# Edge loops of a graph network hand over means in rows of all channels, in place of numerators and denominators

## The chip, the core and the metric

The kernel runs on one core of a Trainium2 chip. The core has five engines with an instruction stream each: TensorE (PE, with its weight loads PEld), VectorE (DVE), ScalarE (ACT), GpSimd (POOL) and SyncE (SP). They work side by side and wait for one another by semaphores. SP issues the ordinary DMAs, POOL the indirect ones that gather rows by index. Time is device microseconds of one execution; lower is better.

## What is computed

10,000 nodes and 160,000 edges with 64 channels each. Four layers of a message-passing network (GENConv with a softmax over the incoming edges of each node, by channel), then one attention layer. What matters here, cut from the reference:

```python
def _genconv(x, src, dst, ea, W1, b1, lg, lb, W2, b2, t):
    m = jax.nn.relu(x[src] + ea) + EPS
    logits = m * t
    mx = jax.ops.segment_max(logits, dst, num_segments=N)
    e = jnp.exp(logits - mx[dst])
    denom = jax.ops.segment_sum(e, dst, num_segments=N)
    alpha = e / denom[dst]
    agg = jax.ops.segment_sum(m * alpha, dst, num_segments=N)
    h = agg + x
    ...
# attention, per edge, 8 heads of 8 channels
score = Kh[src] * Qh[dst] * inv_sqrt_d * Eh
score = jnp.exp(jnp.clip(score.sum(-1, keepdims=True), -5.0, 5.0))
wV = jax.ops.segment_sum(Vh[src] * score, dst, num_segments=n)
```

The edges come sorted by destination, so the edges of a node are neighbours.

## The kernel before

**Layout.** Edges stand along the free dimension, channels on partitions. The edge list is cut in two halves: the first half runs forwards on partitions 0 to 63, the second backwards on 64 to 127. A chunk is 512 columns (`CE`), four groups of 128 columns (`G`), so 1024 edges; there are 158 chunks, the last three short (256, 256 and 128 columns).

**A softmax layer** (`softmax_layer`, four of them; layer 0 also transposes the edge attributes and counts edges per node) goes through the chunks in a loop. Its parts:

- `fetch(k + 3)`: SP loads the marks (two DMAs), and in layers 1 to 3 the edge attributes `ea` (one).
- `front(k)`: POOL gathers the source nodes' rows into `xg`, eight gathers (seven chunk buffers). PE adds edge attributes and gathered rows in a PSUM bank `z`. ACT makes the logits `lg` in two steps (L834, L835). DVE scans them for the running maximum `u` (L841) and subtracts (L843). ACT makes `up` and `e` in three steps (L846, L848, L849).
- `back(k - 1)`, for the chunk before: DVE makes `me` (L869) and scans the running sums `se` of the exponentials (the denominators, L871) and `sm` of the weighted messages (the numerators, L874). Two transposes in blocks of 32x32 (L900) put both in a tile `so`. SP stores it in four DMAs (L904) to the table `st0` in DRAM.
- `decay(k)`: ACT writes `dec` (L856), one PSUM bank, which the scans of `back(k)` read; so it waits for the scan `sm` of chunk k - 1.

At the last edge of each node the running sums are that node's sums; so the table holds a row for every edge, and one row is read for each node. Row 2e + s of `st0` belongs to edge column e of side s and holds 32 denominators and 32 numerators of channels 0 to 31, then the same of channels 32 to 63: 512 bytes, stored in pieces of 256.

`InOrder` ties each engine's instructions to one another in the order in which they are written, so nothing overtakes on an engine.

**The node layer** (`node_layer`) follows each edge loop. `fetch` gathers the rows of 128 nodes a time (79 gathers, in groups of up to eight) by the row numbers `ends`; `divide` forms numerator / denominator as numerator x exp(-ln(denominator)) with two ACT operations and a DVE multiply; `enter` transposes to channels on partitions and adds the layer's input. Then follow two matrix products and two norms, in a software pipeline of groups. `rows_of_nodes` works out `ends` once, during layer 0.

**The attention layer** (`attention_layer`) runs the same chunk loop once more: eight gathers `kv` a chunk, a query scan, scores, weights, a scan `s` (L1201), one transpose to `so` (L1212) and four stores (L1216) to `st1`, in pieces of 128 bytes. Per chunk SP issues eight DMAs there. After it the result rows are gathered from `st1`.

In the layers 1 to 3 the `z` of a chunk lies in one of five PSUM banks; in layer 0 in one of three. `oe` is a bank that the edge loops of layers 1 to 3 use only at their last chunk.

Of the kernel before, what the change touches and what calls it, by code (L numbers as in the profile page):

```python
# [9 lines left out]
F32 = mybir.dt.float32  # L10
# [16 lines left out]
def kernel(ctx: ExitStack, tc: tile.TileContext, a, out):  # L27
# [75 lines left out]
    tables = [dram.tile([NP, D], F32, name=f"table{i}") for i in range(L)]  # L103
    kv_table = dram.tile([NP, D2], F32, name="kv_table")
    qs = dram.tile([2 * HALF + NP + P, D], F32, name="qs")
    st0 = dram.tile([2 * HALF + 1, D2], F32, name="st0")
    st1 = dram.tile([2 * HALF + 1, D], F32, name="st1")

    ends_d = dram.tile([2, HALF], BF, name="ends_d")
    keeps_d = dram.tile([2, HALF], BF, name="keeps_d")  # L110
# [59 lines left out]
    empty = const.tile([1, D2 + D], F32, name="empty")  # L170
    for h in range(2):
        nc.gpsimd.memset(empty[:, h * D:h * D + 32], 1.0)
        nc.gpsimd.memset(empty[:, h * D + 32:(h + 1) * D], -EPS)
    nc.gpsimd.memset(empty[:, D2:], 0.0)
    zeros = const.tile([P, 500], F32, name="zeros")
    nc.gpsimd.memset(zeros, 0.0)
    later.append((st0[2 * HALF:2 * HALF + 1, :], empty[:, 0:D2]))
    later.append((st1[2 * HALF:2 * HALF + 1, :], empty[:, D2:]))

    def load(name, shape, ap):  # L180
        t = const.tile(shape, F32, name=name)
# [314 lines left out]
    def rows_of_nodes(pool, ph):  # L496

        def t(name):
            return pool.tile([P, NT], F32, name="rn_" + name, bufs=1)
        V = nc.vector  # L500
        cnt = t("cnt")
        V.tensor_copy(cnt, ph)
        upto, before = place_nodes(pool, cnt, "ept")
        some = t("some")
        V.tensor_scalar(some, cnt, 0.0, None, op0=OP.is_gt)
        ra, rb, inb = t("ra"), t("rb"), t("inb")
        V.tensor_scalar(inb, before, float(HALF), None, op0=OP.is_ge)
# [36 lines left out]
    def pairs(n):  # L544
        return (n + 1) // 2
# [253 lines left out]

    V, S = nc.vector, nc.scalar  # L800

    def softmax_layer(l, ea_rows=None):

        prev = {}
# [60 lines left out]
        def back(k, z, u, dec, e):  # L865
# [11 lines left out]
            if k == NC - 1:  # L877
# [15 lines left out]
                for i, t in ((1, se), (2, sm)):  # L893
                    V.tensor_mul(far[:, i:i + 1], far[:, i:i + 1], top[:, 3:4])
                    V.scalar_tensor_tensor(t[:D, m - 1:m], fin[:D, i:i + 1], top[:, 2:3],
                                           far[:, i:i + 1], op0=OP.mult, op1=OP.add)

            so = edge.tile([P, CE // 32, 2, 32], F32, name="so", bufs=3)
            for i, t in ((0, se), (1, sm)):
                V.transpose(so[:, :m // 32, i, :], t[:, :m].rearrange("p (b e) -> p b e", e=32))  # L900
# [14 lines left out]
        for k in range(NC):  # L915
# [18 lines left out]
            if l == 1 and k % 4 == 0:  # L934
                clear_queries(k // 4)
            order()
        back(NC - 1, *held)
        order()

    def node_layer(l):  # L940
# [21 lines left out]
        @stage  # L962
# [138 lines left out]

        for g in range(3):
            fetch(g)
        divide(0)
        for i in range(NG2 + (4 if last else 3)):
            span_narrow(i - 3)
            widen(i - 1)
# [5 lines left out]
            spans(i - 1)  # L1113
            relu_narrow(i - 3)
            square(i - 2)
            divide(i + 1)
            back(i - 3)
            root_wide(i - 1)
            leave(i - 3)
# [14 lines left out]
    def attention_layer():  # L1134
# [60 lines left out]
        def back(k, keep, pv, sc):  # L1195
# [8 lines left out]
            if k == NC - 1:  # L1204
# [6 lines left out]
            so = edge.tile([P, CE // 32, 32], F32, name="so1", tag="so", bufs=3)  # L1211
            V.transpose(so[:, :m // 32, :], s[:, :m].rearrange("p (b e) -> p b e", e=32))  # L1212
            rows_out = st1[2 * g0 * G:2 * (g0 + n) * G, :].rearrange(
                "(b e s) (h c) -> s h e b c", e=32, s=2, h=2)
            for q in range(4):
                nc.sync.dma_start(rows_out[q // 2, q % 2], so[q * 32:(q + 1) * 32, :m // 32])  # L1216

        order = InOrder()
        got = [fetch(k) for k in range(2)]
# [2 lines left out]
        for k in range(NC):  # L1222
            kvs = fetch_kv(k)
            if k + 2 < NC:
                got.append(fetch(k + 2))
            pv, psc = scores(k, kvs, made)
            if held is not None:
                back(k - 1, *held)
            held = got[k][0], pv, weights(k, psc)
            if k + 1 < NC:  # L1230
                made = ahead(k + 1, *got[k + 1])
            order()
        back(NC - 1, *held)
        order()

    puts = []
# [69 lines left out]
```

## Time and profile before

| | us |
|---|---|
| median of three runs | 10168.21 (10164.5 to 10176.87) |
| profiled execution, its own time | 10256.79 |
| its span, first to last instruction | 10254.7 |
| softmax layer 0, first to last `lg` on ACT | 176 to 2001 |
| softmax layer 3, last `lg` | 7986 |
| attention, first to last gather | 8301 to 10111 |
| a gather on POOL (L756) | 0.943 busy, 0.30 between two |
| DVE scans of a full chunk | 1.28, 1.27, 1.26 |
| DVE transposes of a full chunk | 0.69, 0.67 |
| ACT operations of a full chunk | 0.55 to 0.75 |
| DMA queue of SP | 2,247,039 packets, 827 MB |

The profile's page gives each engine's busy time, the idle time ahead of each group of instructions with what ended it ("releaser"; "remote" where the profile doesn't know, "issue" where it sees no wait), and the DMA traffic. In the timeline a line holds start, duration, engine, source line, operation, output and inputs, and in brackets the idle time of the engine just before it with its releaser. 67,417 instructions ran.

### The profile page before, as it was taken

Reading aid. Unit: us, or ns where it says so; the run is one execution under the profiler, and the core shown is the slowest. Engines: PE = TensorE matmul, PEld = TensorE weight load, DVE = VectorE, ACT = ScalarE, POOL = GpSimd, SP = SyncE. Lnnn points to the kernel's source line nnn. Section 1 sums busy time; section 2 is a strip of 40 time slices with the busy share of each in tenths; the row PEclk is TensorE's granted clock in tenths of the full one; section 3 lists DMA queues with packets and bytes.
Section 4 is the critical chain, followed back from the end, with each engine's and each line's share of the span. In section 5 each row is a group of like instructions: output and inputs, shape, how many; then the busy total and the mean of one; then the engine's idle time right before and its main releaser. Section 6 shows DMA issues by size and latency. Waiting matters only on the chain. (4 is left out here: it accounts for less than half of the span.)

```text
span 10254.7 us, 67417 instructions
## 1 busy us (share of the span) xinstructions
PE 4014.2 (39%) x15762; PEld 2685.3 (26%) x15762; DVE 5449.4 (53%) x7473; ACT 2805.0 (27%) x4803; POOL 6358.1 (62%) x6760
## 2 busy tenths in 40 slices
PE   3554445443333333433333343333333444444452
PEld 2333333222222221222222221222222233333331
DVE  3777677535555554355555543555555445545453
ACT  2333333333333333333333342333333310000000
POOL 4566666556666665566666646666666456666665
PEclk6666666665555556665666575555555667777776
DMA  3555555524555554244444433444444235555553
GB/s 89 113 125 123 123 124 123 123 59 119 125 125 129 128 124 109 62 102 105 104 104 103 105 78 71 105 105 104 103 104 106 62 92 122 125 123 126 122 128 82
DMA packets 2462634, 1103.63 MB, mean 108 GB/s; under 512 B 2039472, under 2 KB 2254438, under 8 KB 2462239
## 3 DMA queue, kind: packets, MB, share of 16 engines
q1 hardware_dynamic: 2247039, 827.14, 33.8%
q0 software_dynamic: 215200, 272.11, 12.6%
q8 instruction: 140, 2.29, 0.1%
q14 instruction: 255, 2.09, 0.1%
HBM read 626.51 MB, written 471.91 MB: 107 GB/s over the span
## 5 line engine op out<-in xcount | busy, mean ns | idle before, releaser
L756 POOL DMA_INDIRECT xg<-table,idxA x2500 | 2358.6, 943 | 1916.9 <-remote 829.7
L756 POOL DMA_INDIRECT xg<-table,idxB x2500 | 2358.8, 944 | 763.1 <-issue 761.2
L841 DVE TENSOR_TENSOR_SCAN u<-lg,u,marks 128x512 f32<-128x512 f32 (+1 forms) x628 | 798.5, 1272 | 2721.5 <-ACT lg L835 1612.7
L829 PE MATMUL z<-ea,eencW 128*128 128x512 f32 (+1 forms) x892 | 864.3, 1071 | 2137.1 <-DMA ea<-eaT 898.3
L831 PEld LDWEIGHTS z<-ident,xg 128*128 128x128 f32 x3512 | 800.4, 311 | 591.8 <-issue 566.5
L756 POOL DMA_INDIRECT kv<-kv_table,idxA x625 | 589.5, 943 | 439.7 <-remote 220.2
L831 PE MATMUL z<-ident,xg 128*128 128x128 f32 x3512 | 794.5, 395 | 162.0 <-DMA xg<-table,idxB 85.9
L829 PEld LDWEIGHTS z<-ea,eencW 128*128 128x128 f32 x892 | 222.2, 306 | 2231.8 <-issue 1981.7
L871 DVE TENSOR_TENSOR_SCAN se<-dec,se,e 128x512 f32<-128x512 f32 (+1 forms) x628 | 792.2, 1261 | 0.0
L874 DVE TENSOR_TENSOR_SCAN sm<-dec,sm,me 128x512 f32<-128x512 f32 (+1 forms) x628 | 782.3, 1246 | 0.0
L846 ACT ACTIVATE up<-lg 128x512 f32<-128x512 f32 (+1 forms) x632 | 374.3, 592 | 1352.9 <-issue 693.6
L756 POOL DMA_INDIRECT kv<-kv_table,idxB x625 | 589.7, 944 | 191.1 <-issue 190.2
L834 ACT ACTIVATE lg<-z 128x512 f32<-128x512 f32 (+1 forms) x446 | 249.4, 559 | 1555.8 <-remote 1032.3
L1185 PE MATMUL dec<-eq,head_sum 128*128 128x512 f32 (+2 forms) x316 | 237.1, 841 | 931.2 <-DVE eq L1183 887.1
L1192 ACT ACTIVATE sc<-sc 128x512 f32<-128x512 f32 (+1 forms) x158 | 98.7, 625 | 1744.7 <-DVE sc L1191 685.0
L784 PE MATMUL ept<-ident,er 128*64 128x128 f32 x1250 | 269.3, 380 | 752.4 <-ACT ea L788 517.7
L856 ACT ACTIVATE dec<-up 128x512 f32<-128x512 f32 (+1 forms) x632 | 377.1, 597 | 658.8 <-issue 561.0
L756 POOL DMA_INDIRECT n_g<-st,ends x316 | 300.8, 952 | 403.2 <-issue 142.2
L835 ACT ACTIVATE lg<-lg,teps,tcol 128x512 f32<-128x512 f32 (+1 forms) x632 | 471.4, 746 | 21.1
L829 PE MATMUL hist<-ea,eencW 128*128 128x512 f32 x186 | 189.5, 1123 | 709.5 <-DMA ea<-eaT 286.6
L829 PE MATMUL ept<-ea,eencW 128*128 128x512 f32 x186 | 185.5, 1100 | 710.3 <-DMA ea<-eaT 286.4
L1156 DVE TENSOR_TENSOR_SCAN qh<-marks,qh,oe 128x512 f32<-128x512 bf16 (+1 forms) x157 | 198.6, 1265 | 488.6 <-remote 389.8
(285 smaller groups left out, 8704.9 us busy)
## 6 DMA issues: line engine op xcount, KB each, us to landing
st<-so SPq DMA_DIRECT2D x2480, 128.0 KB
ea<-eaT SPq DMA_DIRECT2D x620, 256.0 KB
marks<-ends_d SPq DMA_DIRECT2D x1240, 64.0 KB
st<-so SPq DMA_DIRECT2D x652, 64.0 KB
xg<-table,idxA POOLq DMA_INDIRECT x2500
xg<-table,idxB POOLq DMA_INDIRECT x2500
qs<-zeros SPq DMA_DIRECT2D x40, 1000.0 KB
er<-in_edge_attr_dram SPq DMA_DIRECT2D x310, 128.0 KB
```

The lines of the kernel that those rows point to most:

```text
L756: nc.gpsimd.indirect_dma_start(out=t, out_offset=None, in_=table, in_offset=bass.IndirectOffsetOnAxis(ap=idx, axis=0))
L784: nc.tensor.matmul(pt[:D, g * G:(g + 1) * G], er[:, 0, g, :], ident, start=True, stop=True)
L829: nc.tensor.matmul(z[:, :m], eencW, ea[:, :m], start=True, stop=False)
L831: nc.tensor.matmul(z[:, g * G:(g + 1) * G], xg[:, g, :, :].rearrange("p s d -> p (s d)"), ident, start=False, stop=(g == n - 1))
L834: S.activation(lg[:, :m], z[:, :m], AF.Relu)
L835: S.activation(lg[:, :m], lg[:, :m], AF.Identity, bias=teps[:, l:l + 1], scale=tcol[:, l:l + 1])
L841: V.tensor_tensor_scan(u[:, 1:m + 1], lg[:, :m], marks[:, :m], last, op0=OP.max, op1=OP.add)
L846: S.activation(up[:, :m], lg[:, :m], AF.Relu)
L856: S.activation(dec[:, :m], up[:, :m], AF.Exp, scale=-1.0)
L871: V.tensor_tensor_scan(se[:, :m], dec[:, :m], e[:, :m], prev.get("e", zero1), op0=OP.mult, op1=OP.add)
L874: V.tensor_tensor_scan(sm[:, :m], dec[:, :m], me[:, :m], prev.get("m", zero1), op0=OP.mult, op1=OP.add)
L1185: nc.tensor.matmul(psc[:, :m], head_sum, eq[:, :m], start=True, stop=True)
```

## The change

The tables `st0` and `st1` hold rows of all 64 channels, 256 bytes each. Chunks, sides, 32 columns and 16 blocks of a chunk (`SB`) number the rows so that, for one side and one place within the blocks, the 16 blocks of a chunk are 16 neighbouring rows: a run of 4 KB. A chunk is stored in two DMAs, one for each side, of 32 such runs.

The mean leaves the edge loop: `mean` computes exp(-ln(`se`)) on ACT (into the bank `oe`, in layer 0 into SBUF) and multiplies it with `sm` on DVE, then transposes the product. `send_sums` copies, on ACT, the upper 32 channels of each side from their partitions to those of the lower 32, so that a partition holds whole rows, and issues the stores. In iteration k, `send` handles chunk k - 3 and `mean` chunk k - 2, both ahead of `back(k - 1)`. In attention only `send` is there. `divide` disappears from the node layer, whose gathers are 256 bytes a row. `rows_of_nodes` translates `ends` into the new row numbers. A spare part of the tables holds the rows for nodes without edges.

```diff
-    st0 = dram.tile([2 * HALF + 1, D2], F32, name="st0")
-    st1 = dram.tile([2 * HALF + 1, D], F32, name="st1")
+    NB = -(-HALF // CE)
+    SB = CE // 32
+    st0 = dram.tile([NB * 64 * SB, D], F32, name="st0")
+    st1 = dram.tile([NB * 64 * SB, D], F32, name="st1")
...
+        part, upper_part = pool.tile([P, NT], I32, name="rn_part", bufs=1), t("upper")
+        place = t("place")
+        V.tensor_single_scalar(part, ends, 10, op=OP.logical_shift_right)
+        V.tensor_scalar(place, part, float(64 * SB), None, op0=OP.mult)
+        for down, keep, times in ((0, 1, 32 * SB), (1, 31, SB), (6, SB - 1, 1)):
+            of = ends
+            if down:
+                V.tensor_single_scalar(part, ends, down, op=OP.logical_shift_right)
+                of = part
+            V.tensor_single_scalar(part, of, keep, op=OP.bitwise_and)
+            V.tensor_copy(upper_part, part)
+            V.scalar_tensor_tensor(place, upper_part, float(times), place, op0=OP.mult, op1=OP.add)
+        V.tensor_copy(ends, place)
...
+    def turn_sums(t, m):
+        so = edge.tile([P, SB, 2, 32], F32, name="so", bufs=3)
+        V.transpose(so[:, :m // 32, 0, :], t[:, :m].rearrange("p (b e) -> p b e", e=32))
+        return so
+
+    def send_sums(k, so, st):
+        g0, n = chunks[k]
+        nb, b0 = n * G // 32, g0 * G // 32 % SB
+        rows_of = st.rearrange("(k s e b) d -> k s e b d", s=2, e=32, b=SB)[g0 * G // CE]
+        for s in range(2):
+            p = s * D
+            S.activation(so[p:p + 32, :nb, 1, :], so[p + 32:p + D, :nb, 0, :], AF.Copy)
+            nc.sync.dma_start(rows_of[s, :, b0:b0 + nb, :],
+                              so[p:p + 32, :nb].rearrange("p b h c -> p b (h c)"))
...
-            so = edge.tile([P, CE // 32, 2, 32], F32, name="so", bufs=3)
-            for i, t in ((0, se), (1, sm)):
-                V.transpose(so[:, :m // 32, i, :], t[:, :m].rearrange("p (b e) -> p b e", e=32))
-            rows_out = st0[2 * g0 * G:2 * (g0 + n) * G, :].rearrange(
-                "(b e s) (h x) -> s h e b x", e=32, s=2, h=2)
-            for q in range(4):
-                nc.sync.dma_start(rows_out[q // 2, q % 2],
-                                  so[q * 32:(q + 1) * 32, :m // 32].rearrange("p b i c -> p b (i c)"))
+            summed.append((k, se, sm))
+
+        def mean():
+            if summed:
+                k, se, sm = summed.pop(0)
+                m = span(k)[1] * G
+                r = ps("oe", [P, CE]) if ph is None else edge.tile([P, CE], F32, name="r", tag="me", bufs=1)
+                S.activation(r[:, :m], se[:, :m], AF.Ln)
+                S.activation(r[:, :m], r[:, :m], AF.Exp, scale=-1.0)
+                mn = edge.tile([P, CE], F32, name="mn")
+                V.tensor_mul(mn[:, :m], sm[:, :m], r[:, :m])
+                turned.append((k, turn_sums(mn, m)))
+
+        def send():
+            if turned:
+                send_sums(*turned.pop(0), st0)
...
             if counts and counts[-1][-1] == R * KT:
                 rows_of_nodes(edge, ph)
+            send()
+            mean()
             if held is not None:
                 back(k - 1, *held)
...
+        send()
+        mean()
         back(NC - 1, *held)
+        send()
+        mean()
+        send()
...
-            my["g"] = t = edge.tile([P, GRP, D2], F32, name="n_g", tag="so", bufs=3)
+            my["h"] = t = edge.tile([P, GRP, D], F32, name="n_g", tag="so", bufs=3)
...
-        def divide(my, g, i0, n, c):
-            q = 2 * pairs(n)
-            t = my["g"][:, :q].rearrange("p n (h i c) -> p n h i c", h=2, i=2)
-            my["h"] = h = work.tile([P, GRP, D], F32, name="n_h", bufs=2)
-            S.activation(t[:, :, :, 0, :], t[:, :, :, 0, :], AF.Ln)
-            S.activation(t[:, :, :, 0, :], t[:, :, :, 0, :], AF.Exp, scale=-1.0)
-            V.tensor_mul(h[:, :q, :].rearrange("p n (h c) -> p n h c", h=2), t[:, :, :, 1, :], t[:, :, :, 0, :])
...
             pv, psc = scores(k, kvs, made)
+            send()
             if held is not None:
                 back(k - 1, *held)
```

In `attention_layer` the four stores after the transpose give way to `turned.append((k, turn_sums(s, m)))` in the same manner.

More of the change, by code (lines that the diff above doesn't have):

```diff
@@ L169 @@
     nc.vector.memset(neg1, NEG)
[L170 to L174, printed above, removed]
+    empty = const.tile([64, 2 * D], F32, name="empty")
+    nc.gpsimd.memset(empty[:, :D], -EPS)
+    nc.gpsimd.memset(empty[:, D:], 0.0)
     zeros = const.tile([P, 500], F32, name="zeros")
     nc.gpsimd.memset(zeros, 0.0)
-    later.append((st0[2 * HALF:2 * HALF + 1, :], empty[:, 0:D2]))
-    later.append((st1[2 * HALF:2 * HALF + 1, :], empty[:, D2:]))
+    assert HALF % CE
+    used = HALF // 32 % SB
+    for i, st in enumerate((st0, st1)):
+        later.append((st.rearrange("(k p b) d -> k p b d", p=64, b=SB)[NB - 1, :, used:, :],
+                      empty[:, None, i * D:(i + 1) * D].to_broadcast([64, SB - used, D])))
     def load(name, shape, ap):
@@ L800 @@
     V, S = nc.vector, nc.scalar
+    def turn_sums(t, m):
[5 more added lines that the diff above has]
+        nb, b0 = n * G // 32, g0 * G // 32 % SB
+        assert b0 + nb <= SB
+        rows_of = st.rearrange("(k s e b) d -> k s e b d", s=2, e=32, b=SB)[g0 * G // CE]
[4 more added lines that the diff above has]
+                              so[p:p + 32, :nb].rearrange("p b h c -> p b (h c)"))
     def softmax_layer(l, ea_rows=None):
@@ L896, in back @@
                                            far[:, i:i + 1], op0=OP.mult, op1=OP.add)
-            so = edge.tile([P, CE // 32, 2, 32], F32, name="so", bufs=3)
-            for i, t in ((0, se), (1, sm)):
-                V.transpose(so[:, :m // 32, i, :], t[:, :m].rearrange("p (b e) -> p b e", e=32))
-            rows_out = st0[2 * g0 * G:2 * (g0 + n) * G, :].rearrange(
-                "(b e s) (h x) -> s h e b x", e=32, s=2, h=2)
-            for q in range(4):
-                nc.sync.dma_start(rows_out[q // 2, q % 2],
-                                  so[q * 32:(q + 1) * 32, :m // 32].rearrange("p b i c -> p b (i c)"))
+            summed.append((k, se, sm))
[12 more added lines that the diff above has]
+                send_sums(*turned.pop(0), st0)
+        summed, turned = [], []
         order = InOrder()
@@ L960, in fetch @@
                 V.memset(t[:, n, :], 1.0)
-        @stage
-        def divide(my, g, i0, n, c):
-            q = 2 * pairs(n)
-            t = my["g"][:, :q].rearrange("p n (h i c) -> p n h i c", h=2, i=2)
-            my["h"] = h = work.tile([P, GRP, D], F32, name="n_h", bufs=2)
-            S.activation(t[:, :, :, 0, :], t[:, :, :, 0, :], AF.Ln)
-            S.activation(t[:, :, :, 0, :], t[:, :, :, 0, :], AF.Exp, scale=-1.0)
-            V.tensor_mul(h[:, :q, :].rearrange("p n (h c) -> p n h c", h=2), t[:, :, :, 1, :], t[:, :, :, 0, :])
         @stage
@@ L1103, in node_layer @@
             fetch(g)
-        divide(0)
         for i in range(NG2 + (4 if last else 3)):
@@ L1115, in node_layer @@
             square(i - 2)
-            divide(i + 1)
             back(i - 3)
@@ L1210, in back, with send @@
                                        op0=OP.mult, op1=OP.add)
[L1211 to L1216, printed above, removed]
+            turned.append((k, turn_sums(s, m)))
+        turned = []
+        def send():
+            if turned:
+                send_sums(*turned.pop(0), st1)
         order = InOrder()
@@ L1232, in attention_layer @@
             order()
+        send()
         back(NC - 1, *held)
+        send()
         order()
```

## The prediction

> **What bounds the kernel now.** I read the page's busy shares first, then busy time by stretches, then POOL's timeline, then one chunk's timeline in a softmax layer. Busy shares:
>
> ```profile
> PE 4014.2 (39%) x15762; PEld 2685.3 (26%) x15762; DVE 5449.4 (53%) x7473; ACT 2805.0 (27%) x4803; POOL 6358.1 (62%) x6760
> ```
>
> No engine is near full, so waits decide. Two stretches of 1400 us inside layers 1 and 2, instructions on the gathered tile `xg` alone; the columns behind the length are PE, PEld and POOL busy (count), granted clock, DMA share, GB/s:
>
> ```profile
> 2400.00:3800.00 1400.00, 227.35 (x984) 234.06 (x984) 929.59 (x986) 0.56 0.52 126
> 4400.00:5800.00 1400.00, 230.52 (x988) 238.81 (x989) 931.77 (x988) 0.61 0.46 104
> ```
>
> Eight gathers make a chunk, so 1400/986 x 8 = 11.36 us a chunk in layer 1 and 11.34 in layer 2. Layer 1 moves a fifth more bytes (the zeros for `qs`) at the same pace: DMA load doesn't set it. The same division gives 11.75 for layer 0 (817 gathers from 600 to 1800 us) and 11.6 for attention (1034 from 8500 to 10000). POOL in layer 2:
>
> ```profile
> 5207.36 0.94 POOL L756 DMA_INDIRECT xg<-table,idxB  x1 [0.30 <-issue]
> 5216.96 0.94 POOL L756 DMA_INDIRECT xg<-table,idxA  x1 [8.66 <-remote]
> ...
> 5275.63 0.94 POOL L756 DMA_INDIRECT xg<-table,idxB  x1 [0.30 <-issue]
> 5285.20 0.94 POOL L756 DMA_INDIRECT xg<-table,idxA  x1 [8.63 <-remote]
> ```
>
> Gathers follow each other every 1.248 us, 9.98 a chunk; after 48 of them (six chunks) POOL waits 8.6 us for a free `xg`, and 5285.20 - 5216.96 = 68.24 = 6 x 11.37. ACT's next `lg` starts at 5216.73, beside POOL's release: both wait for PE, whose matmuls the trace shows done long before. I can't name what holds PE's signal back; the trace shows only that it clears some 8 us after POOL stops. So POOL with this stall sets the pace, and DVE and ACT must merely be faster than 11.37. Are they? One chunk, nothing late:
>
> ```profile
> 5223.67 0.55 ACT L834 ACTIVATE lg<-z 128x512 f32<-128x512 f32 x1
> 5224.26 0.75 ACT L835 ACTIVATE lg<-lg,teps,tcol 128x512 f32<-128x512 f32 x1
> 5225.04 1.28 DVE L841 TENSOR_TENSOR_SCAN u<-lg,u,marks 128x512 f32<-128x512 f32 x1 [0.71 <-ACT lg L835]
> 5226.36 0.70 DVE L843 TENSOR_TENSOR lg<-lg,u 128x512 f32<-128x512 f32 x1
> 5226.97 0.68 DVE L869 SCALAR_TENSOR_TENSOR me<-z,e 128x512 f32<-128x512 f32 x1
> 5227.09 0.60 ACT L846 ACTIVATE up<-lg 128x512 f32<-128x512 f32 x1 [2.09 <-DVE lg L843]
> 5227.56 1.27 DVE L871 TENSOR_TENSOR_SCAN se<-dec,se,e 128x512 f32<-128x512 f32 x1
> 5227.59 0.59 ACT L848 ACTIVATE e<-lg 128x512 f32<-128x512 f32 x1
> 5228.21 0.63 ACT L849 ACTIVATE e<-e 128x512 f32<-128x512 f32 x1
> 5228.76 1.26 DVE L874 TENSOR_TENSOR_SCAN sm<-dec,sm,me 128x512 f32<-128x512 f32 x1
> 5229.93 0.69 DVE L900 STREAM_TRANSPOSE so<-se 128x512 f32<-128x512 f32 x1
> 5230.05 0.60 ACT L856 ACTIVATE dec<-up 128x512 f32<-128x512 f32 x1 [1.21 <-issue]
> 5230.54 0.67 DVE L900 STREAM_TRANSPOSE so<-sm 128x512 f32<-128x512 f32 x1
> 5230.58 0.55 ACT L834 ACTIVATE lg<-z 128x512 f32<-128x512 f32 x1
> ...
> 5231.95 1.28 DVE L841 TENSOR_TENSOR_SCAN u<-lg,u,marks 128x512 f32<-128x512 f32 x1 [0.71 <-issue]
> ```
>
> A ring between two engines, each in written order: scan `u`, subtract, `me`, `se`, `sm` on DVE; then `dec` on ACT, which needs `sm`'s end because `dec` is one bank; then the next `lg`, twice, and the next `u`. It takes 5231.95 - 5225.04 = 6.91 us. The margin to POOL's 11.37 is 4.46 us, and 3.07 to 9.98.
>
> **The change, part by part.** The decisive part is where `send` and `mean` stand: after `front(k)`, ahead of `back(k - 1)`. ACT's order becomes `lg`, `lg`, `up`, `e`, `e`, two copies (`send`), Ln, Exp (`mean`), `dec`. DVE's becomes `u`, subtract, multiply `mn`, one transpose, `me`, `se`, `sm`. The multiply needs this iteration's Exp, and `me`, `se` and `sm` are queued behind it on DVE; `dec`, the next `lg` and, through the z banks, PE and then POOL wait for those.
>
> From the start of `u` as 0, with the spacings of the fence: subtract 1.32 to 2.02; `up` 2.05; `e` 2.55; its exponent 3.17. New from here: copies at 3.70 and 4.23 (0.53 is the spacing from `dec` to `lg`; they have 32 partitions, but 512 elements each like the rows here), Ln at 4.76, Exp at 5.38 (0.62 as between the dependent `e` steps), ending at 6.01. Multiply at 6.04 (0.69, as the subtract), transpose at 6.77, `me` 7.38, `se` 7.97, `sm` 9.17, ending at 10.43. `dec` 10.46, `lg` 11.00 and 11.59, ending 12.34, next `u` at **12.37**. DVE does the same amount as before (a multiply for a transpose); what is added is 5.46 us in which DVE waits for ACT. The margin of 4.46 is used up: the ring, not POOL, sets the pace of layers 1 to 3.
>
> Layers 1 to 3: ACT's first `lg` to its last took about 1805 us (6181 to 7986 in layer 3). New: 155 full chunks x 12.37 = 1917, some 20 for the three short ones, and the start. In layer 2's start ACT began chunks at 4206.31, 4232.90, 4260.90, and chunk 7 only at 4329.35, 145 us after chunk 0 at 4184.1, held by PE's late signal. Seven turns of the new ring are 87, so 58 are lost; the old ring of 6.91 caught up later, the new one can't. That loss lies between 0 (should the lateness come from the stores) and 58; I take 58, as POOL's order is unchanged. 1917 + 20 + 58 - 1805 = +190 a layer, **+570**.
>
> Layer 0: ACT's copy of `ea` (L788) stands before `send`, +0.53, so `sm` ends at 10.96; then four one-hot operations on DVE take 2.2 us (1016.11 to 1018.33 between the first and the next `u`) against 1.94 on ACT: 13.2 us a chunk for 139 chunks, 12.9 for 16, 20 for the rest: 2061 against 11.75 x 156 = 1833, **+230**. ACT's waits for PE at `ea` (510.7 us in the whole layer, 3.3 a chunk) now lie inside the ring: between 0 and +510. I take 0: POOL, at 13.2 a chunk, will stand still 3.2 us in each, about as long as the 3.7 after which such a wait ends now.
>
> Stores: of 2048 packets a chunk in four issues, 64 runs in two issues stay, and half the bytes in the softmax layers. I cost that at nothing there: POOL's gathers and then the ring hide it. In attention two of eight SP issues and 2048 short packets go; ACT, with one operation a chunk, has room for two copies, whose transpose was made an iteration earlier, so nothing waits for them. Attention stays on POOL: between 0 and 156 x (11.6 - 9.98) = -250 if the stalls were the stores' fault. I take 0, because layers 1 and 2 show the pace insensitive to DMA load and the node stage, without these stores, has the same late signals (DVE L1026 waited 16.92 us at 6053.03).
>
> The Trainium skill's DMA: Bandwidth & Descriptors (Specifications) asks for at least 512 B a transfer, below which the engine reads, modifies and writes. By it the 2048 short writes are the thing to remove. If they set the pace, five stages would go at POOL's 9.98, some 1170 us less; the two stretches above say that they don't.
>
> Node stages: Ln, Exp and multiply (0.63 + 0.63 + 0.69) leave the path of the first group, and gathers stay 0.94 on POOL whatever their length. At the layer's end Ln, Exp, multiply and copies on the last short chunk come ahead of the last store: about 0.3 each, +2. These cancel: 0, within 10 either way. `rows_of_nodes` gains 14 operations on 128x79, about 0.2 each: +3, once.
>
> **Sum**, against the profiled execution (span 10254.7, time 10256.8): 570 + 230 + 3 = +803. The median of the runs is 88.6 below that execution; applied to it: 10168 + 803 = 10971, say **10970 us**.
>
> **The rivals.** *Slower, but the stores did cause part of the lateness*: the start loss goes (-174) and attention gains 250; 803 - 424 = +379, 10550. For it: SP's issues crawl at times (four stores took 4.25 us at 5210.97 and 2.17 at 5231.24). Against: equal pace at unequal load. *Slower still*: PE's late signals hit the ring as well, +510 in layer 0 and 5% of 1917 in three layers: +1600, 11770; half of it, about 11370, is likelier, since POOL now idles more. *Faster*: the ring doesn't decide, because Ln and Exp overlap DVE's work and the turn stays below 11.3; then only attention's stall, ended by the missing stores, shows: 10168 - 250 = 9920. Its place is `mean`'s multiply, its price 5.46 us, and it decides once the wait for Exp is under 4.4. Against: the written order on both engines, which the fence shows kept. *No change*: the ring stays hidden and attention too, 10170; it needs the same.
>
> **How the numbers follow.** Forecast 0.53, milder 0.20, stronger 0.17, faster 0.07, no change 0.03. The forecast's own range is 10750 to 11200 (start loss halved; a third of the extra waits). Down to the milder case and up to half of the stronger one: **10550 to 11380**. A measurement can tell 0.2%, 20 us, from no change. Faster 0.07, same 0.03, slower 0.90.
>
> **What would show it.** Right: in layers 1 to 3 a turn from `u` to `u` of 12.3 to 12.5, with DVE waiting about 4 us for ACT's Exp before each `mn`; POOL idle 2.4 us a chunk or more; 13 and more in layer 0; attention near 11.6. Wrong: turns near 7 with DVE unhindered, or attention's chunk at 10. The forecast falls with the step that has the multiply wait for the same iteration's Exp.

## The result, and the profile after

The changed kernel takes **11254.5 us** (median of 4 runs, 11250.3 to 11257.9) where the kernel before, run beside it, takes 10167.3: a ratio of 1.107, 95% interval 1.105 to 1.109, or +1087 us. The forecast was 10,970 in a range of 10,550 to 11,380. The profiled execution has a span of 11251.3 us.

The head of the page, the DMA queue of SP and the chain of waits of the changed kernel:

```profile
PE 4030.1 (36%) x15762; PEld 2695.1 (24%) x15762; DVE 5535.6 (49%) x7439; ACT 4476.7 (40%) x7551; POOL 6366.8 (57%) x6757
...
q1 hardware_dynamic: 673883, 663.59, 20.3%
...
DVE 27%; ACT 25%; issue 23%; PE 9%; another core or an unknown queue 8%; DMA 4%; POOL 2%; SPq 2%; DVEq 0%; ACTq 0%; POOLq 0%
```

What the change says of the stores is true: 2,247,039 packets of SP's queue became 673,883. Yet the kernel is slower, and every engine but ACT has a smaller share of the span than before. ACT works 1672 us more (4476.7 against 2805.0), DVE 86 us more: no engine came near full. The chain is half DVE and ACT in turns. That is a ring, and one chunk of layer 2 shows it (start, duration, engine, line and operation, idle time before it and what ended that):

```profile
5203.26 1.28 DVE L879 TENSOR_TENSOR_SCAN u<-lg,u,marks 128x512 f32<-128x512 f32 x1 [1.90 <-ACT lg L873]
5204.51 0.94 POOL L776 DMA_INDIRECT xg<-table,idxA  x1 [3.11 <-PE z L869]
5204.58 0.70 DVE L881 TENSOR_TENSOR lg<-lg,u 128x512 f32<-128x512 f32 x1
5205.31 0.60 ACT L884 ACTIVATE up<-lg 128x512 f32<-128x512 f32 x1 [2.08 <-DVE lg L881]
...
5206.43 0.63 ACT L887 ACTIVATE e<-e 128x512 f32<-128x512 f32 x1
...
5207.08 1.28 ACT L836 ACTIVATE so<-so 32x512 f32<-32x512 f32 x2
...
5208.38 0.60 ACT L943 ACTIVATE oe<-se 128x512 f32<-128x512 f32 x1
...
5209.02 0.58 ACT L944 ACTIVATE oe<-oe 128x512 f32<-128x512 f32 x1
...
5209.63 0.69 DVE L946 TENSOR_TENSOR mn<-sm,oe 128x512 f32<-128x512 f32 x1 [4.35 <-ACT oe L943]
...
5210.99 0.65 DVE L907 SCALAR_TENSOR_TENSOR me<-z,e 128x512 f32<-128x512 f32 x1
...
5212.75 1.25 DVE L912 TENSOR_TENSOR_SCAN sm<-dec,sm,me 128x512 f32<-128x512 f32 x1
...
5213.31 2.05 PE L867 MATMUL z<-ea,eencW 128*128 128x512 f32 x2 [9.07 <-DMA ea<-eaT]
...
5214.03 0.60 ACT L894 ACTIVATE dec<-up 128x512 f32<-128x512 f32 x1 [4.44 <-DVE u L878]
...
5214.57 0.55 ACT L872 ACTIVATE lg<-hist 128x512 f32<-128x512 f32 x1
...
5215.94 1.28 DVE L879 TENSOR_TENSOR_SCAN u<-lg,u,marks 128x512 f32<-128x512 f32 x1 [1.90 <-ACT lg L873]
```

From `u` to `u` 5215.94 - 5203.26 = 12.68 us. DVE stands 4.35 us ahead of the product `mn`, because ACT goes through `up`, twice `e`, the two copies, Ln and Exp first; then ACT stands 4.44 us ahead of `dec`, because `me`, `se` and `sm` were queued behind that product. The first wait is new; the second was 1.21 us in the prediction's lines. POOL, which set the pace, now waits some 3 us in every chunk for PE (3.11 here). The next `lg` on ACT follows `dec` without idle time, so PE isn't a part of the ring: it follows it. The profile puts most of PE's wait (2226 of 2601 us before this matmul) down to the load of `ea`, which SP issues behind the stores, and SP waits 4159 us in all for ACT's copies. In a stretch inside layer 2 (columns as in the prediction: PE, PEld, POOL busy on `xg`, clock, DMA share, GB/s), POOL makes 780 gathers in 1200 us, 65 fewer than the 845 that 986 in 1400 us were (the stretch still holds a part of the layer's start, in which POOL runs ahead); the DMA share fell from 0.46 to 0.30:

```profile
4800.00:6000.00 1200.00, 172.31 (x731) 176.13 (x730) 735.50 (x780) 0.57 0.30 72
```

Where the time went, from the first to the last scan `u` of each layer (`s` in attention), in us of the two profiled executions (that of the kernel before was 88.6 us over the median of its runs):

| stage | before | after | difference | predicted |
|---|---|---|---|---|
| layer 0 | 1823.6 | 2137.4 | +314 | +230 |
| layer 1 | 1810.5 | 2041.4 | +231 | +190 |
| layer 2 | 1804.4 | 2041.4 | +237 | +190 |
| layer 3 | 1804.3 | 2041.3 | +237 | +190 |
| attention | 1783.6 | 1790.4 | +7 | 0 |
| all else | 1228.3 | 1199.4 | -29 | +3 |
| span | 10254.7 | 11251.3 | +997 | +803 |

### The profile page after: what moved, and what is told of

It is laid out like the page before. It is cut to its first block, busy times and chain, and to the rows that moved or that the text cites. A ratio compares the mean times of both kernels' runs of the same rounds, so it can differ in the third digit from the quotient of the medians.

```text
span 11251.3 us, 69225 instructions
## 1 busy us (share of the span) xinstructions
PE 4030.1 (36%) x15762; PEld 2695.1 (24%) x15762; DVE 5535.6 (49%) x7439; ACT 4476.7 (40%) x7551; POOL 6366.8 (57%) x6757
## 4 chain that ended last, share of the span: by engine, by line
DVE 27%; ACT 25%; issue 23%; PE 9%; another core or an unknown queue 8%; DMA 4%; POOL 2%; SPq 2%; DVEq 0%; ACTq 0%; POOLq 0%
ACT so L836 7%; DVE u L879 6%; DVE sm L912 5%; DVE so L825 3%; DVE lg L881 3%; ACT up L884 3%; ACT lg L873 3%; ACT dec L894 2%; ACT e L886 2%; DVE me L907 2%; ACT oe L943 2%; ACT lg L872 2%; DMA ea<-eaT 2%; PE z L867 2%
## 5 line engine op out<-in xcount | busy, mean ns | idle before, releaser
L776 POOL DMA_INDIRECT xg<-table,idxA x2500 | 2362.4, 945 | 2636.0 <-PE z L869 1199.4
L867 PE MATMUL z<-ea,eencW 128*128 128x512 f32 (+1 forms) x892 | 899.2, 1112 | 2601.0 <-DMA ea<-eaT 2226.2
L946 DVE TENSOR_TENSOR mn<-sm,oe 128x512 f32<-128x512 f32 (+1 forms) x474 | 323.1, 682 | 2033.5 <-ACT oe L943 1056.5
L836 ACT ACTIVATE so<-so 32x512 f32<-32x512 f32 (+1 forms) x1580 | 982.8, 622 | 43.1 <-DVE so L825 2.8
L869 PEld LDWEIGHTS z<-ident,xg 128*128 128x128 f32 x3512 | 836.2, 324 | 588.3 <-issue 559.7
L869 PE MATMUL z<-ident,xg 128*128 128x128 f32 x3512 | 825.6, 409 | 122.9 <-DMA xg<-table,idxB 79.1
L946 DVE TENSOR_TENSOR mn<-sm,r 128x512 f32<-128x512 f32 (+1 forms) x158 | 108.4, 686 | 767.6 <-issue 349.1
```

The source lines that it names most:

```text
L776: nc.gpsimd.indirect_dma_start(out=t, out_offset=None, in_=table, in_offset=bass.IndirectOffsetOnAxis(ap=idx, axis=0))
L836: S.activation(so[p:p + 32, :nb, 1, :], so[p + 32:p + D, :nb, 0, :], AF.Copy)
L867: nc.tensor.matmul(z[:, :m], eencW, ea[:, :m], start=True, stop=False)
L869: nc.tensor.matmul(z[:, g * G:(g + 1) * G], xg[:, g, :, :].rearrange("p s d -> p (s d)"), ident, start=False, stop=(g == n - 1))
L946: V.tensor_mul(mn[:, :m], sm[:, :m], r[:, :m])
```

## The experiments

The runs met two kinds of chips, and this has to be known to read them. On one the kernel before takes some 10,180 us, as in the first measurement; on the other 8762 to 8777. In the traces of the second kind, all of changed versions, POOL's gathers go on without the stalls of 8 us; the kernel before was timed there, but left no trace. "With stalls" and "without" below mean these; each run is compared with the kernel before on its own chip. A chip was met at one time only, so whether the chip makes the difference or something of that time can't be told apart. e2, e3, e5, e7, e8 and e11 are single runs, the others medians of 2 to 10.

| run | what | stalls | us | before | turn of `u`, layers 1 to 3 (median; mean of turns 20 to 150) |
|---|---|---|---|---|---|
| e1 | product a turn later | no | 8789.5 | 8776.8 | 9.8 to 9.9 |
| e2 | old stores added | no | 10604.2 | 8776.8 | 12.68 |
| e3 | Ln twice | no | 11008.9 | 8776.8 | 13.3 |
| e4 | spread | no | 8768.6 | 8776.8 | 9.8 to 10.0 |
| e5 | as before | yes | 10174.2 | 10182.2 | 6.91, mean 11.26 |
| e6 | as changed | yes | 11261.8 | 10182.2 | 12.68 |
| e7 | means, then copies | yes | 10414.4 | 10182.2 | 11.25 |
| e8 | both behind `decay` | yes | 10297.3 | 10182.2 | 9.56, mean 11.29 |
| e9 | spread | no | 8753.5 | 8761.9 | 9.8 to 9.9 |
| e10 | spread, 9 buffers | no | 8752.7 | 8761.9 | 9.7 to 9.9 |
| e11 | spread, 4 buffers | no | 8753.0 | 8761.9 | 9.8 to 9.9 |
| e12 | spread, 9 buffers | yes | 10262.8 | 10184.4 | 7.04, mean 11.23 |

**e1: the wait alone taken away.** All operations, stores and their places stay; DVE's product takes the reciprocal that ACT made an iteration earlier. In layer 0 the reciprocal also gets a buffer of its own, in place of one that it shared with `me` (not shown).

```diff
         def mean():
+            if logged:
+                k, sm, r = logged.pop(0)
+                m = span(k)[1] * G
+                mn = edge.tile([P, CE], F32, name="mn")
+                V.tensor_mul(mn[:, :m], sm[:, :m], r[:, :m])
+                turned.append((k, turn_sums(mn, m)))
             if summed:
...
                 S.activation(r[:, :m], r[:, :m], AF.Exp, scale=-1.0)
-                mn = edge.tile([P, CE], F32, name="mn")
-                V.tensor_mul(mn[:, :m], sm[:, :m], r[:, :m])
-                turned.append((k, turn_sums(mn, m)))
+                logged.append((k, sm, r))
```

> Every operation of the change and its place in the chunk are kept, only the product takes the Exp of the iteration before, so that DVE no longer waits for ACT there. Theory (that wait lengthened the ring of DVE and ACT): DVE's seven operations end at about 6.4 us after u, ACT's nine at 6.4, dec and the two lg follow, and the ring turns in 8.4 us, below POOL's 9.98. Layers 1 to 3 go back to some 1805 us from first to last u (2041 now), layer 0 to about 1830 (2137 now), and the time to about 10,150 (10,100 to 10,250). Rival 1 (the amount of ACT and DVE work, or the new form of the stores, is what costs): all of that is still there, so the time stays at 11,250. Rival 2 (the old stores had made PE's signals late, the ring hides it now): turns fall below 11.3 towards 9.98, and the time below 9,900.

Measured: 8789.5 us against 8776.8 for the kernel before, ratio 1.0015 (1.0005 to 1.0025). ACT is as busy (4500 us) and DVE too (5483 us), the stores are the new ones, and nearly the whole price is gone. The two engines no longer take turns:

```profile
4017.03 0.68 DVE L943 TENSOR_TENSOR mn<-sm,oe 128x512 f32<-128x512 f32 x1
...
4018.93 1.28 ACT L836 ACTIVATE so<-so 32x512 f32<-32x512 f32 x2
4018.95 1.26 DVE L909 TENSOR_TENSOR_SCAN se<-dec,se,e 128x512 f32<-128x512 f32 x1
...
4020.14 1.25 DVE L912 TENSOR_TENSOR_SCAN sm<-dec,sm,me 128x512 f32<-128x512 f32 x1
4020.23 0.60 ACT L949 ACTIVATE oe<-se 128x512 f32<-128x512 f32 x1
...
4020.86 0.58 ACT L950 ACTIVATE oe<-oe 128x512 f32<-128x512 f32 x1
...
4021.42 0.60 ACT L894 ACTIVATE dec<-up 128x512 f32<-128x512 f32 x1
```

`mn` begins with no idle time, and `se` and `sm` on DVE run beside the copies, Ln and Exp on ACT. Rival 1, the amount of work, falls. The time that theory gave (10,150) was for the other kind of chip; what it said of the change, that the price goes, came in. Taken by its numbers, rival 2 (turns near 9.98, under 9,900 us) came in too, but the kernel before with its old stores was as fast here, so this run doesn't speak for it; e8 decides on it.

**e2: the old stores added.** Four issues a chunk, 2048 runs of 256 B, go to a tensor that nobody reads.

```diff
+                for q in range(4):
+                    p = q // 2 * D
+                    nc.sync.dma_start(rows_out[q // 2, q % 2],
+                                      so[p:p + 32, :m // 32].rearrange("p b i c -> p b (i c)"))
```

> The changed kernel with four more stores a chunk in layers 0 to 3, 2048 runs of 256 B to a tensor that nobody reads, beside the new ones. Theory (the ring of 12.68 us sets the pace, and packets are hidden): the turn stays 12.68, the time 11,255 within 60. Rival 2 (short stores make PE's signals late): POOL's stalls of 8.6 us after 48 gathers come back on top, some 1 us a chunk or more, 11,700 and above. Rival 3 (the ring's length comes from the ACT copies waiting for the stores' buffers): more stores hold so longer, and the turn grows by the four issues, at 0.7 us each 2.8 us a chunk, 13,000.

Measured: SP's queue moved 1,994,331 packets, three times those of the changed kernel, and the turn is the same 12.68 us to the hundredth; the wait too:

```profile
5019.38 0.94 POOL L777 DMA_INDIRECT xg<-table,idxA  x1 [3.14 <-PE z L870]
...
5021.47 0.69 DVE L947 TENSOR_TENSOR mn<-sm,oe 128x512 f32<-128x512 f32 x1 [4.35 <-ACT oe L945]
```

Short stores cost nothing in this ring, and rival 3 falls. Nor did they bring stalls of POOL to this chip, as rival 2 had it. The time expected, 11,255, was for a chip with stalls. The 10,604 us against 8777 (one run) is also the nearest that the runs come to the change's price without stalls: +1827 us, 21%. The changed kernel itself was not run on such a chip. Its layers 1 to 3 show the start loss: 1978, 1977 and 1978 us at the same turn, 64 less than the 2041 with stalls.

**e3: Ln twice.**

```diff
                 S.activation(r[:, :m], se[:, :m], AF.Ln)
+                S.activation(r[:, :m], se[:, :m], AF.Ln)
```

> Ln is computed twice, one after the other, in the same place. Theory (everything that ACT does between e and the product lies in the ring): each turn grows by one ACT operation, 0.62 to 0.65 us, to 13.3 in layers 1 to 3, and layer 0 by as much; 4 x 155 x 0.63 = 390 more, 11,645. Rival (the ring has slack, something else sets 12.68): 11,255 unchanged.

Measured: turns of 13.32 us in layers 1 to 3, 0.64 more than 12.68, and 14.12 in layer 0 for 13.46. The wait ahead of `mn` grew from 4.35 to 4.98 us:

```profile
5714.58 0.69 DVE L947 TENSOR_TENSOR mn<-sm,oe 128x512 f32<-128x512 f32 x1 [4.98 <-ACT oe L945]
```

So each ACT operation between `e` and the product is in the ring at its full spacing. The sum of 11,645 was for the chip with stalls; here it is 11,009, and 11,009 - 4 x 155 x 0.64 = 10,612 agrees with e2.

**e4: the work spread.** Ln and Exp, now in a function `logs`, stand in `front` behind the second `lg`, `send` stays, and product and transpose stand behind `back`:

```diff
             S.activation(lg[:, :m], lg[:, :m], AF.Identity, bias=teps[:, l:l + 1],
                          scale=tcol[:, l:l + 1])
+            logs()
...
             send()
-            mean()
             if held is not None:
                 back(k - 1, *held)
+            mean()
```

> The same work, laid where the engines waited in the kernel before: Ln and Exp stand on ACT behind the second lg, while DVE scans u and subtracts (2.0 us free); the copies stay between e and dec (1.2 us free); product and transpose stand on DVE behind the sm scan, where the two transposes stood. Theory: the ring turns in about 7.0 us, POOL's gathers with their stalls set the pace as before, 11.3 a chunk; the node stages keep what they gained (29 us between the layers), so 10,140 (10,080 to 10,200), 0 to 0.8% under the kernel before. Rival 1 (work or the stores' form costs): near 11,250. Rival 2 (the old stores were the cause of PE's late signals): pace 10 to 10.5 a chunk, 9,400 to 9,700.

Measured: 8768.6 us against 8776.8, ratio 0.9990 (0.9980 to 0.9999). Busy time on `xg` in a stretch of layer 2:

```profile
3700.00:5000.00 1300.00, 389.84 (x1040) 258.70 (x1040) 983.01 (x1040) 0.52 0.37 92
```

One chunk of the same layer in the timeline:

```profile
4012.59 0.59 ACT L944 ACTIVATE oe<-se 128x512 f32<-128x512 f32 x1
4012.70 1.28 DVE L880 TENSOR_TENSOR_SCAN u<-lg,u,marks 128x512 f32<-128x512 f32 x1 [3.84 <-ACT lg L873]
...
4017.59 0.66 DVE L954 TENSOR_TENSOR mn<-sm,oe 128x512 f32<-128x512 f32 x1
...
4020.84 0.58 ACT L872 ACTIVATE lg<-z 128x512 f32<-128x512 f32 x1 [2.41 <-PE z L869]
```

1040 gathers in 1300 us are 10.0 us a chunk with nothing between them but POOL's own 0.30; Ln runs beside `u`, the product follows `sm` at once, and ACT's next `lg` waits for PE and so for POOL. The numbers expected (10,140, or 9,400 to 9,700 for rival 2) supposed stalls, and I had not reckoned with a chip without them; the kernel before was as fast there, so that this run says nothing on the stalls' cause. Rival 1 falls again.

**e5 and e6: the two kernels again.**

> The kernel before, for its trace beside the runs of this call. The last call's times of it were 8776.8 against 10168 in the first measurement, and the kernels there gathered without the stalls of 8.6 us. Theory (POOL sets the pace, the stalls came from outside the kernel): where the time is near 8777, POOL issues a gather every 1.248 us without stalls, 9.98 to 10.0 us a chunk in layers 1 to 3 and in attention, and PE's signals come within 1 us of its last matmul; where it is near 10,168, the stalls are back, 11.3. Rival (the old stores make the stalls): stalls and 11.3 a chunk in either case, and a time near 8777 would have to come from elsewhere.

> The changed kernel, beside the same before. Theory: the ring of 12.68 us depends on nothing outside DVE and ACT, so layers 1 to 3 keep 12.68 a turn and layer 0 13.5 wherever it runs, and start and attention get faster by the missing stalls: 155 x 12.68 + 14 = 1979 in layers 1 to 3, 2125 in layer 0, attention 1560; with 8777 for the kernel before 10,600 (10,560 to 10,640), with 10,168 again 11,255. Rival (the ring's length comes from late signals): turns shorter than 12.68 where there are no stalls.

This chip stalls: 10,174 and 11,262 us, ratio of the second 1.106 (1.103 to 1.109). In the kernel before POOL waits 8.2 us after each 48 gathers:

```profile
4639.64 0.94 POOL L756 DMA_INDIRECT xg<-table,idxA  x1 [8.19 <-remote]
...
4707.49 0.94 POOL L756 DMA_INDIRECT xg<-table,idxA  x1 [8.24 <-remote]
```

The time expected for the changed kernel with stalls was 11,255. Its turn is 12.68 us here, in the first measurement, and in e2 on a chip without stalls: the ring does not know what POOL does. By stage this pair says more than the first, since both executions lie near their medians: layer 0 takes 345 us longer, layers 1 to 3 243 to 248 each, attention 33, and all else gives 22 back.

**e7: means, then copies.** `mean` stands ahead of `send`.

```diff
-            send()
             mean()
+            send()
```

> send and mean change places: Ln and Exp stand right behind e, the two copies behind them, while DVE multiplies and scans. Theory (the copies are in the ring because they stand ahead of Ln): the turn loses their 1.28 us, 12.68 to 11.40; DVE still waits for Exp, 3.1 us. 4 x 155 x 1.28 = 790 less: 9,810 where the kernel before takes 8777; where it takes 10,168, POOL's 11.3 with its stalls takes over, about 10,350 to 10,500. Rival (copies cost by what they do and not by where they stand): unchanged against the changed kernel.

Measured: 10,414 us, 847 less than the changed kernel beside it, from two steps that changed places. The copies moved out of the wait:

```profile
4656.93 0.63 ACT L887 ACTIVATE e<-e 128x512 f32<-128x512 f32 x1
4657.47 0.58 ACT L943 ACTIVATE oe<-se 128x512 f32<-128x512 f32 x1
...
4658.70 0.69 DVE L946 TENSOR_TENSOR mn<-sm,oe 128x512 f32<-128x512 f32 x1 [2.91 <-issue]
...
4660.17 1.28 ACT L836 ACTIVATE so<-so 32x512 f32<-32x512 f32 x2 [1.50 <-DVE mn L946]
...
4661.81 1.25 DVE L912 TENSOR_TENSOR_SCAN sm<-dec,sm,me 128x512 f32<-128x512 f32 x1
```

They run while DVE scans. The turn is 11.25 us, 1.43 less: Ln follows `e` after 0.54 us instead of 1.95 (8.38 - 6.43 in the fence of the result). That is next to POOL's pace with stalls, 11.3, and the mean turn is 11.32. The range expected, 10,350 to 10,500, held.

**e8: both behind `decay`.**

```diff
-            send()
-            mean()
             if held is not None:
                 back(k - 1, *held)
             held = z, u, decay(k, up), e
+            send()
+            mean()
```

> send and mean stand behind back and decay. DVE's product then waits for an Exp that stands ahead of the next lg, and nothing of back is queued behind it. Theory: u to sm 5.0 us as in the kernel before, dec to 5.6, copies to 6.9, Ln and Exp to 8.15, two lg, next u at 9.5: under POOL's 9.98, so layers 1 to 3 go at POOL's pace. In layer 0 the one-hot operations are queued behind the product (8.9) and the transpose (9.5) on DVE, 2.2 us: 11.7 to 12.3 a turn, over POOL's pace by 1.7 to 2.3, 270 to 360 us. In all 9,030 to 9,140 where the kernel before takes 8777. Rival (any place costs, the work is the price): above 10,000.

Measured: 10,297 us, 115 over the kernel before. The turn is 9.56 us where nothing holds it (expected 9.5), 11.83 in layer 0 (expected 11.7 to 12.3; one-hot operations are queued behind the product there). Against e5 layer 0 takes 63 us longer, layers 1 to 3 23 to 26 each, attention 36, and all else 48 less. The time expected, 9,030 to 9,140, was for a chip without stalls; the mark of the rival that any place costs, 10,000, is passed here by the kernel before too. This run settles the rival that short stores make PE late. It issues five DMAs a chunk on SP for the old seven and has no short stores in the edge loops, yet POOL stalls as in e5: 846 gathers in 1200 us of layer 2 against 848, at DMA shares of 0.32 and 0.44. Busy time on `xg` in that stretch, e5:

```profile
4600.00:5800.00 1200.00, 197.81 (x848) 203.97 (x848) 799.28 (x848) 0.57 0.44 104
```

The same stretch of e8:

```profile
4600.00:5800.00 1200.00, 198.53 (x848) 204.59 (x848) 799.15 (x846) 0.56 0.32 81
```

And two of POOL's waits in e8, 48 gathers apart:

```profile
4759.99 0.95 POOL L776 DMA_INDIRECT xg<-table,idxA  x1 [8.12 <-remote]
...
4827.87 0.95 POOL L776 DMA_INDIRECT xg<-table,idxA  x1 [8.16 <-remote]
```

**e9 to e12: can the spread version win where there are stalls?** It was run again, with 9 buffers for the gathered rows, and with 4 (`bufs=9` and `bufs=4` in place of `bufs=7` on `xg`, `kv` and `n_kvq`).

> The spread version once more, since its first run met a chip on which the kernel before takes 8777 us, and its bound there is POOL without stalls. Where the kernel before takes 10,170 to 10,180: theory: the ring turns in 7 us, POOL's 9.98 and its stalls, 8.2 us after every 48 gathers, set 11.3 a chunk in layers 1 to 3; the node stages save some 25 us, attention gives back 10 to 20 (11.65 against 11.5 a chunk), so 10,150 (10,100 to 10,220). Rival (the old stores caused the stalls): 10 to 10.5 a chunk and 9,600 or less.

> The spread version with 9 buffers for the gathered rows instead of 7 (kv of attention has the same buffers). If a stall of POOL has a fixed length of 8.2 us and comes once in (buffers - 1) chunks, it goes from 8.2 / 6 = 1.37 to 8.2 / 8 = 1.03 us a chunk: 0.34 x 155 x 3 = 160 less in layers 1 to 3, with attention some 200 less than the spread version. If the stall grows with the time that POOL ran without one, its share stays and the time is that of the spread version within 30. Where there are no stalls (8777 for the kernel before), no difference in either.

> The spread version with 4 buffers for the gathered rows. If a stall has a fixed length of 8.2 us and comes once in 3 chunks: 2.7 a chunk, pace 12.7, some 900 more than the spread version with attention. If its length grows with the time that POOL ran without one: the same pace with shorter stalls, within 100 of the spread version. Without stalls (8777 for the kernel before): four buffers still cover landing and matmuls, within 30.

The chip had no stalls: 8753.5, 8752.7 and 8753.0 us against 8761.9, the first two at a ratio of 0.9991 (0.9981 to 1.0000). Four buffers are enough, and nothing is learnt of the stalls.

> The spread version with 9 buffers once more, for a chip on which POOL stalls (10,170 to 10,180 for the kernel before). Theory: the ring turns in 7 us and is hidden. With stalls of fixed length once in 8 chunks the pace is 9.98 + 8.2 / 8 = 11.0 in layers 1 to 3 (11.3 with 7 buffers), and the time some 9,950 to 10,050; with a stall that grows with the time without one, 11.3 and 10,100 to 10,200. Rival (the old stores caused the stalls): 10 to 10.5 and 9,600 or less. Where the kernel before takes 8760 to 8777: 10.0 a chunk and 0.1% under it, as in the last call.

This one met a chip with stalls, and both of my accounts of them missed: 10,262.8 us, 0.75% over the kernel before, ratio 1.0075 (1.0058 to 1.0092): clear of noise, if small. POOL's waits come after 48 gathers with 9 buffers as with 7, not after 64, and are about as long, 8.1 to 8.7 us in layer 2:

```profile
4774.30 0.94 POOL L776 DMA_INDIRECT xg<-table,idxA  x1 [8.66 <-remote]
...
4842.03 0.94 POOL L776 DMA_INDIRECT xg<-table,idxA  x1 [8.12 <-remote]
```

The pace is that of e5, 11.23 for 11.26. The 99 us between the two profiles (10,271.4 against 10,172.3) lie elsewhere: each of layers 0 to 3 takes 23 to 25 us longer and attention 36, and all else gives 31 back. In layer 1 POOL's gathers take about as long (1772 and 1768 us), but the last `u` begins 63 us after the last gather, for 44 in e5. In layers 1 to 3 the first 20 turns take 26 to 27 us more than in e5 and the rest 3 to 5 less: turns of 28 us, that of the start with stalls, go on for a chunk or two longer, and there are two buffers more. That points to the buffers, but isn't shown, since the spread version with 7 was not run here. In e8, with 7 buffers, the last `u` lags by 68 us, but its turn is 9.56 for 7.04, so it can't clear the buffers. Attention is longer by 28 to 36 us in e6, e7 and e8 too, with 7 buffers; why stays open. So no version beats both kernels everywhere: the spread one is within 0.2% of the kernel before without stalls, and its form with 9 buffers 0.75% over it with stalls; it stays well under the changed one with stalls, and under e2, which stands for it, without.

## Why the prediction was right, point by point

**The range: in part luck.** The step that decides came in as described, but 11,254 lies 284 us over the forecast and outside the forecast's own range of 10,750 to 11,200. It lies in the stated range because that was widened upwards for half of the stronger rival, which did not occur. Of the 284 us, 194 net are terms of the sum and 90 the median on which the sum was set; both follow.

**The product's wait for this iteration's Exp: right.** DVE waits 4.35 us ("about 4"), POOL stands 3.1 us a chunk ("2.4 or more"), turns don't vary. e1 takes that one wait away and the price goes; e3 lengthens it by one operation and the turn grows by 0.64. The way on to POOL was named as the z banks; the profile puts most of PE's wait down to the load of `ea` instead (see the result). `me`, which frees a bank, ends 1.4 to 2 us before PE starts in that stretch, so the trace doesn't settle which of the two holds PE. Both follow the ring, and the time is the same.

**The ring's 12.37 us: one term mis-sized.** It is 12.68. From `u`, the prediction had the copies at 3.70, Ln at 4.76, the product at 6.04, `dec` at 10.46; measured are 3.82, 5.12, 6.37 and 10.77. All of the 0.31 arises up to Ln: the copies begin 0.12 later, and two of them take 1.30 for the 1.06 predicted. It is one term, taken three times: I took 0.53 as the spacing at a copy, from the step of `dec` to `lg`; from `e` to the first copy, to the second and to Ln it is 0.65 each. A copy of 32 partitions is busy for 0.62 us, no less than the operations of 128 partitions beside it (0.55 to 0.63, the second `lg` apart). The later steps are right within 0.03. Times 155 this is 48 us a layer, the difference of 41 to 47 between 190 and the measured 231 to 237.

**The start loss of 58: right.** 2041.4 - 155 x 12.68 = 76 for the start and the three short chunks, that is 56 at the predicted 20. The first turns are as late as before although the stores are new (10, 16, 28, 27, 28, 22 us), and where nothing stalls (e2) 64 us less are needed.

**Layer 0: right in kind, 84 short.** The layer took 2137 us for the 2061 of the working, and the kernel before 1824 for its 1833. Of the 76, some 35 are the copies again: 122 turns of 13.46 for the predicted 13.2, and 14 near the end of 13.25 for 12.9. The rest are turns that the working did not single out: 10 us in those up to 14.22 with `encode_columns`, 24 around one of 33.4 with `fold_weights`, 9 in one of 22.6 with `rows_of_nodes`. That ACT's waits for PE at `ea` would not come into the ring (0 of up to 510) held: they fell from 511 to 76 us.

**Attention and the stores at nothing: right against the -250, not quite nothing.** Attention took 7 us more in the first pair, but 33 more in e6 than in e5, on one chip; no run shows why. The rule of the Trainium skill against short transfers, DMA: Bandwidth & Descriptors (Specifications), finds no effect in these runs: e2 adds 2048 writes of 256 B a chunk and the turn stays 12.68; e4 has none of them in its edge loops and is 0.1% from the kernel that has them. The stores are behind other work in both.

**Node stages at 0 within 10: 29 us off**, on the gaining side. The four gaps behind the layers shrank by 1 to 14 us; I did not follow why by so unequal amounts.

**Sum and median: the 90 us.** 803 was made against a profiled execution that was 88.6 us above its median, and set on the median. In the profiles +997 was measured, in the medians +1087: that execution was the odd one, not the changed kernel's, which is at its median. In the next pair (e5, e6) the spans differ by 1094.

**The rivals.** The milder one, that short stores made PE late, falls with e8: stalls without them. The stronger one, late signals in the ring, falls with turns that are 12.68 throughout. The faster one needed an overlap that e1 had to build first. What the prediction took for the kernel's own pace, 11.37, comes with the stalls: without them POOL goes at the 9.98 that the text had as its lower bound, the margin is 3.07 for 4.46, and the change costs 2.7 us a chunk instead of 1.4.

## What to carry to other kernels

Where two engines hand a chunk back and forth in written order, what an operation costs depends on its place: ahead of a wait between the engines it costs its whole spacing in every turn (0.64 us for the second Ln), in a gap nothing. Without stalls the same Ln, Exp, copies and product cost some 1830 us where they stand ahead of the scans (e2, with the old stores added), and once each stands in a gap that the profile shows, nothing: the spread version is 0.1% under the kernel before. With stalls its form with 9 buffers is 0.75% over it. Before moving work into such a loop, write the turn down from `u` to `u`, put each new operation at its time, and look at what is queued behind the one that waits. And do not spend two engines on a transfer that already lies behind a third: count what sets the pace first.

## What the runs showed of the hardware

One program has two paces. The kernel before took 10,164 to 10,196 us in the first measurement (10,257 in its profiled execution) and on two chips, and 8759 to 8779 us on two others, each met at one time. Where it is slow, POOL pauses 8.1 to 8.8 us after each 48 gathers in layer 2, and 1 to 4 us after one or two chunks in attention; ACT's and POOL's next instructions start together when a pause ends (5216.73 and 5216.96 in the prediction's lines). By the trace the matmuls were long done by then: past the start of layers 2 and 3 of e5, ACT's waits of over 3 us ahead of the first `lg` end 18 to 31 us after the chunk's last matmul, in e4 without stalls within 0.1 us of it. Stores (64 or 2048 runs a chunk), SP's issues (5 or 7) and buffers (7 or 9) change neither the 48 nor, by more than some 0.5 us, the length. In about half of the cases an issue or a semaphore step of SP takes 0.69 to 0.73 us in layers 1 to 3 then (e5 and e8); without stalls the median issue takes 0.45 (e4). In the changed kernel (e6) longer pauses (6.7 us after 40 gathers, 279 us into layer 2) and slow steps go on while POOL still runs ahead of the ring, for some 430 us, 40 chunks, into layers 2 and 3; from there on POOL waits 3 us in each chunk and both are gone. No run shows what causes them.
